# Seven block products for the output projection of a head pair, with the output's sums kept transposed in DRAM

## The chip, the cores and the metric

The kernel runs on one core of a Trainium2 chip. The metric is the device time in microseconds. A core has TensorE (PE, matmuls), VectorE (DVE), ScalarE (ACT), GpSimd (POOL) and SyncE (SP), each with its own stream of instructions that it works through in order. DMAs are issued from the streams of SP, ACT and POOL. SBUF is the on-chip memory of 128 partitions, PSUM the memory that TensorE writes, in 8 banks of 512 f32 columns.

## The reference

One block of a transformer on x of 2048 tokens by 256, all f32:

```python
xn = layernorm(x)                                   # over the 256
q, k, v = split(xn @ Wqkv.T)                        # 16 heads of 128 each
w = softmax(q @ k.T * 128 ** -0.5)                  # per head, 2048 x 2048
attn = concat_heads(w @ v) @ Wout.T                 # 2048 x 2048 -> 2048 x 256
ffn = (sigmoid(xn @ Q(w1).T) * (xn @ Q(w2).T)) @ Q(w3).T   # Q: weights to -1, 0, 1
out = x + attn + ffn
```

Softmax divides by a sum over keys; a kernel may divide after the product with V.

## The kernel before

**Tiling.** Tokens are cut into NB = 4 blocks of QB = 512; a block has TB = 4 tiles of 128 queries. A group is G = 2 heads. The attention runs over 64 blocks, block n being head n // 4, token block n % 4 (`blocks`, L586). The order of all instructions is written out by hand (`tc.manual_schedule()`, L732): each pass of the loop at L733 is a step, with u = 4n + t. A step computes scores for tile v = u + 6 (`scores`, L589) and a quarter of the weighted sum of block n (`weighted`, L652).

**A step.** TensorE makes 4 score matmuls into two PSUM tiles "s" (three exist), VectorE takes the row maxima (L607, L612), ScalarE the exps with their sums (L619). `exchanged` (L625) moves exps between partitions by 16 DMAs, 10 on SP's queue and 6 on ACT's; two steps later VectorE transposes 32x32 blocks (`transposed`, L645, L650) into pT. TensorE adds up V times pT over 16 key tiles in one PSUM bank "av" (L660), 4 of them a step. At the block's end ScalarE copies av to oT (L672).

**Products in between.** Q, K and V of later heads are made while attention runs. They come as a block matrix product of 2x2 blocks done by seven products of blocks instead of eight, from sums of weights (`weight_sums`, `v_sums`, on POOL) and of x (`x_sums`). A product is one matmul of 128x128 by 128x512 (L165, L263) into the single PSUM bank "m"; VectorE adds it into one or two results (L185 to L192, L280). In a step the first product follows the scores and its reads follow the maxima; the second follows two or three matmuls of the weighted sum and is read after the transposes. Steps t = 2, 3 do Q and K of the next head, steps t = 0 do V of the next group. V is exchanged between partitions by POOL's DMAs (L287) and transposed by VectorE (L295).

**The projection.** In step t = 1 `projected` (L676) multiplies the former block's oT, 128 queries at a time, by the head's 128x256 slice of Wout: four matmuls of 256 columns, a head at a time. VectorE scales each by the softmax's reciprocal (`inverses`, L639) and adds it into y, the running output of the token block, in one instruction (L693). y stands as [token, 256] in SBUF for one block and in DRAM between (`fetched` L715, `put_away` L721, POOL's queue).

**The front.** FFN results come out transposed (yT, L497). `added` (L500) turns them back by TensorE's transposes (L512) and adds x (L516).

Of the kernel before, what the change touches and what calls it, by code (L numbers as in the profile page):

```python
# [8 lines left out]
F32 = mybir.dt.float32  # L9
# [10 lines left out]
def layernorm_attention_bitffn_kernel(  # L20
# [51 lines left out]
    def load_weights(g: int, what: str, queue=nc.sync):  # L72

        if what == "o":
            w = wpool.tile([P, G, DM], F32, tag="wo", name=f"wo{g}")
            src = woutT[g * G * D : (g + 1) * G * D, :].rearrange("(h p) e -> p h e", p=P)
        else:
            w = wpool.tile([P, KC, G * D], F32, tag=f"w{what}", name=f"w{what}{g}")
            lo = "qkv".index(what) * HD + g * G * D
            src = wqkvT[:, lo : lo + G * D].rearrange("(c p) e -> p c e", p=P)  # L80
        queue.dma_start(w, src)
        weights[g, what] = w
# [131 lines left out]
    VH = NV // 2  # L214

    def v_piece(g: int, i: int):
# [9 lines left out]
        v = v_tile(g, i // VH).rearrange("p g k d -> p k g d")  # L226
        i = i % VH * 2
        nc.scalar.copy(v[:, i : i + 2], pm.rearrange("p k (g d) -> p k g d", g=G))

    def v_tile(g: int, half: int):  # L230
        if (g, half) not in vs:
            vs[g, half] = kvpool.tile(
                [P, G, NKT // 2, D], F32, tag="v", name=f"v{g}_{half}", bufs=4
            )
        return vs[g, half]
# [5 lines left out]
    def v_sums(g: int):  # L241
        wv = weights[g, "v"]
        w = wpool.tile([P, 4, D], F32, tag="wvs", name=f"wvs{g}")
        a, b = wv[:, :, :D], wv[:, :, D:]
        nc.gpsimd.tensor_tensor(w[:, 0], b[:, 0], b[:, 1], ALU.add)
        nc.gpsimd.tensor_tensor(w[:, 1], w[:, 0], a[:, 0], ALU.subtract)
        nc.gpsimd.tensor_tensor(w[:, 2], a[:, 0], b[:, 0], ALU.subtract)
        nc.gpsimd.tensor_tensor(w[:, 3], a[:, 1], w[:, 1], ALU.subtract)
        vws[g] = w

    def fast_v_product(g: int, m: int, second: bool):
        half, m = divmod(m, NB)
        wv, w, t = weights[g, "v"], vws[g], ts[2 * half]
# [3 lines left out]
            ((wv[:, 0, :D], x00), (w[:, 1], t[:, 1])),  # L257
            ((w[:, 2], t[:, 2]), (wv[:, 1, D:], t[:, 3])),
            ((w[:, 0], t[:, 0]), (w[:, 3], x11)),
            ((wv[:, 1, :D], x10),),  # L260
# [4 lines left out]

    def fast_v_read(g: int, m: int, second: bool, pm):
        half, m = divmod(m, NB)
        v = v_tile(g, half).rearrange("p g k d -> p g (k d)")
        a, b = (v[:, i].rearrange("p (j k r) -> p k j r", j=P // 32, r=32) for i in range(G))
        a0, a1, b0, b1 = a[:, :TB], a[:, TB:], b[:, :TB], b[:, TB:]  # L270
        pm = pm.rearrange("p (k j r) -> p k j r", j=P // 32, r=32)
        if (m, second) == (0, False):
            nc.vector.tensor_copy(a0, pm)
            return
        todo = {
            (0, True): ((a1, a0),), (1, False): ((b1, a1),), (1, True): ((b0, b1),),
            (2, False): ((b1, b1), (a1, a1)), (2, True): ((a1, a1),), (3, False): ((a0, a0),),
# [4 lines left out]
    def v_exchanged(g: int, half: int, i: int):  # L282

        v = v_tile(g, half)[:, i].rearrange("p k d -> p (k d)")
# [7 lines left out]
    def v_transposed(g: int, half: int, i: int):  # L292
        v = v_tile(g, half)[:, i].rearrange("p k (q r) -> p q k r", r=32)
# [5 lines left out]
    vws, v_part = {}, [xnT[:, 0, bass.ts(c, QB)] for c in (1, 3)]  # L299
# [5 lines left out]

    ys = [fw.tile([P, TB, DM], F32, tag=f"y{c}", name=f"y{c}") for c in range(NB)]
    away = ctx.enter_context(tc.tile_pool(name="away", bufs=1, space=bass.MemoryType.DRAM))
    yds = [away.tile([P, TB, DM], F32, tag=f"yd{c}", name=f"yd{c}") for c in range(NB)]  # L310


    def loads(fraw):
# [33 lines left out]
        for what in "ko":  # L347
            load_weights(0, what)
# [130 lines left out]
    def summed(fp, c: int, f: int):  # L479
# [14 lines left out]
        if f == FC - 1:  # L494
            yT = fp.tile([P, DM // P, QB], F32, tag="yT", name=f"yT{c}", bufs=1)
            for e in range(DM // P):
                nc.scalar.copy(yT[:, e], yTs[c][e])  # L497
            yTs[c] = yT

    def added(c: int):  # L500

        yT = yTs.pop(c)
        if c < NB - 1:
            pt = ps_s.tile([P, 2, QB], F32, tag="s", name=f"pyt{c}")
            pts = [pt.rearrange("p a (b e) -> p (a b) e", e=DM)]
        else:
            pts = [bank([P, 2, DM], f"pyt{c}_{u}") for u in range(2)]
        m = TB // len(pts)
        for u, pt in enumerate(pts):
            for t in range(m):  # L510
                for e in range(DM // P):
                    nc.tensor.transpose(  # L512
                        pt[:, t, bass.ts(e, P)], yT[:, e, bass.ts(u * m + t, P)], ident
                    )
            y = ys[c][:, u * m : (u + 1) * m]
            nc.vector.tensor_tensor(y, pt, y, ALU.add)  # L516
        nc.sync.dma_start(yds[c], ys[c])


    with tc.manual_schedule():  # L520
# [45 lines left out]
        for i, (c, f) in enumerate(chunks):  # L566
# [7 lines left out]
            if f == 3 and c:  # L574
                added(c - 1)
# [11 lines left out]
    sums, rinvs, oTs, exps, parts, pTs, avs = {}, {}, {}, {}, {}, {}, {}  # L587

    def scores(v: int, amid=None, late=None):  # L589

# [8 lines left out]
        for i in range(2):  # L599
# [9 lines left out]
            if i == 0 and amid:  # L609
                amid()  # L610
# [28 lines left out]
    def inverses(n: int):  # L639
# [3 lines left out]
        rinvs[n] = ri  # L643
# [8 lines left out]
    def weighted(n: int, k: int, part=None):  # L652
# [3 lines left out]
        if k == 0:  # L656
# [4 lines left out]
            av, vs[h // G, k // (NKT // 2)][:, h % G, k % (NKT // 2), :],  # L661
# [3 lines left out]
        if k == NKT - 1:  # L665
            oT = apool.tile([P, QB], F32, tag="oT", name=f"oT{n}_{t0}", bufs=1)
            if part == 1:

                nc.vector.tensor_copy(oT[:, :P], av[:, :P])  # L669
                nc.scalar.copy(oT[:, P : 2 * P], av[:, P:])  # L670
            else:
# [216 lines left out]
```

## Time and profile before

| | |
|---|---|
| median of 3 runs | 2254.63 us (2254.19 to 2256.97) |
| the profiled execution's own time | 2257.09 us |
| its span, first to last instruction | 2255.3 us |
| granted TensorE clock | 0.999 |
| PE, DVE, ACT, POOL busy | 2244.7, 1681.3, 692.8, 317.8 us |
| step with scores and weighted sum alone | 6.87 us |
| projection matmuls | 256 of 128x256 |
| q0 (POOL's DMAs), share of 16 DMA engines | 12.0% |

The profile names instructions by engine, line of the kernel and tiles (out<-in, buffer numbers left out). A group's row has busy time, mean ns of one, and the idle time of its engine before it with what ended that. Matmuls are pipelined: the length of one is longer than the distance to the next, so costs on TensorE are read from start to start. A timeline row gives start, length, engine, line, operation, count.

### The profile page before, as it was taken

The numbers are of one execution on the slowest core, as the hardware profiler recorded it, in microseconds if no ns is written. First come the engines' busy times: TensorE is split into PE (matmuls) and PEld (weight loads), VectorE is DVE, ScalarE is ACT, GpSimd is POOL, SyncE is SP. The second block draws the span as 40 slices with busy tenths as digits, with TensorE's granted clock in tenths as the row PEclk, the third lists the DMA queues.
The fourth block names the chain that finished last, engine by engine and source line by source line (L and its number), as shares of the span: only waits on it lengthen the run. The fifth ranks groups of instructions, "written<-read, shape, count | busy, mean of one in ns | idle before, by whom it ended". The sixth has DMA issues, their size and how long they took to land.

```text
span 2255.3 us, 24534 instructions
## 1 busy us (share of the span) xinstructions
PE 2244.7 (100%) x5754; PEld 1086.1 (48%) x5754; DVE 1681.3 (75%) x2205; ACT 692.8 (31%) x1203; POOL 317.8 (14%) x625
## 2 busy tenths in 40 slices
PE   9999999999999999999999999999999999999999
PEld 6744444444444444444444444444444444444445
DVE  6566777777777777777777777777777777777775
ACT  5533323223223223323323322322322322232331
POOL 0010000021030211203022120222103021120000
PEclk9999999999999999999999999999999999999999
DMA  2066665665665665666666665666666666666665
GB/s 95 28 164 160 171 162 147 175 176 151 166 182 152 180 174 149 177 173 167 160 175 157 176 181 147 166 179 173 168 159 174 166 174 164 157 176 173 168 170 155
DMA packets 237793, 364.73 MB, mean 162 GB/s; under 512 B 74576, under 2 KB 82192, under 8 KB 237648
## 3 DMA queue, kind: packets, MB, share of 16 engines
q1 hardware_dynamic: 131120, 178.36, 31.9%
q10 hardware_dynamic: 74704, 101.68, 17.8%
q0 software_dynamic: 31824, 83.13, 12.0%
q8 instruction: 45, 0.74, 0.1%
q14 instruction: 100, 0.82, 0.1%
HBM read 46.20 MB, written 35.65 MB: 36 GB/s over the span
## 4 chain that ended last, share of the span: by engine, by line
PE 94%; DMA 2%; SPq 1%; DVE 1%; ACT 1%; issue 0%; ACTq 0%; DVEq 0%
PE s L602 37%; PE av L660 37%; PE pw L165 7%; PE po L686 5%; PE pvw L263 3%; DMA part<-p 2%; PE ph L467 2%; PE pv L222 1%; PE pf L490 1%; SPq L634 1%; ACT p L619 0%; PE pq L115 0%; DVE pT L650 0%; PE pk L105 0%; ACTq L634 0%
## 5 line engine op out<-in xcount | busy, mean ns | idle before, releaser
L619 ACT ACTIVATE p<-s,nm 128x1024 f32<-128x1024 f32 x512 | 566.0, 1110 | 1436.8 <-DMA part<-p 986.3
L607 DVE TENSOR_REDUCE mx<-s 128x1 f32<-128x1024 f32 x512 | 626.8, 1225 | 448.8 <-PE s L602 448.6
L660 PE MATMUL av<-pT,v 128*128 128x512 f32 (+1 forms) x2080 | 940.2, 586 | 0.7 <-DVE pT L650 0.7
L602 PE MATMUL s<-kT,qT 128*128 128x512 f32 x2048 | 921.9, 592 | 1.6 <-ACT p L619 1.5
L650 DVE STREAM_TRANSPOSE pT<-part 128x1024 f32<-128x1024 f32 x512 | 604.8, 1219 | 29.4 <-DMA part<-p 27.6
L660 PEld LDWEIGHTS av<-pT,v 128*128 128x128 f32 x2080 | 395.1, 190 | 456.3 <-issue 449.9
L602 PEld LDWEIGHTS s<-kT,qT 128*128 128x128 f32 x2048 | 388.6, 190 | 464.8 <-issue 452.5
L287 POOL DMA_DIRECT2D xnT<-v x384 | 189.2, 501 | 346.5 <-DVE v L295 236.4
L721 POOL DMA_DIRECT2D yd<-ya x60 | 33.6, 560 | 735.3 <-DVE ya L693 734.0
L686 PE MATMUL po<-wo,oT 128*128 128x256 f32 x512 | 131.7, 380 | 0.6 <-DVE oT L669 0.5
L686 PEld LDWEIGHTS po<-wo,oT 128*128 128x128 f32 x512 | 97.0, 190 | 67.8 <-issue 58.4
L693 DVE SCALAR_TENSOR_TENSOR ya<-po,ri,ya 128x256 f32<-128x256 f32 x256 | 111.9, 479 | 18.0 <-issue 2.5
L619 ACT ACTIVATION_READ_ACCUMULATOR p<-s,nm 128x1 f32 x512 | 100.2, 196 | 0.0
L165 PE MATMUL pw<-t,ws 128*128 128x512 f32 x168 | 85.9, 593 | 0.0
L715 POOL DMA_DIRECT2D ya<-yd x64 | 34.3, 536 | 306.4 <-DMA yd<-ya 238.5
L188 DVE TENSOR_TENSOR kT<-pw,kT 128x512 f32<-128x512 f32 x112 | 74.7, 667 | 0.2 <-issue 0.2
L612 DVE TENSOR_REDUCE nm<-mx 128x1 f32<-128x2 f32 x256 | 39.7, 155 | 28.2 <-DVE mx L607 1.4
L185 DVE SCALAR_TENSOR_TENSOR qT<-pw,qT 128x512 f32<-128x512 f32 x84 | 57.4, 684 | 0.0
L165 PE MATMUL pw<-xnT,wk 128*128 128x512 f32 x112 | 57.2, 592 | 0.0
L280 DVE TENSOR_TENSOR v<-pvw,v 128x512 f32<-128x512 f32 x84 | 56.1, 680 | 0.0
L672 ACT COPY oT<-av 128x512 f32<-128x512 f32 x64 | 37.3, 583 | 59.2 <-PE av L660 53.6
L165 PEld LDWEIGHTS pw<-t,ws 128*128 128x128 f32 x168 | 31.6, 189 | 40.7 <-issue 33.7
(113 smaller groups left out, 784.8 us busy)
## 6 DMA issues: line engine op xcount, KB each, us to landing
part<-p SPq DMA_DIRECT2D x2560, 64.0 KB, 2.1
part<-p ACTq DMA_DIRECT2D x1536, 64.0 KB, 2.2
ya<-yd POOLq DMA_DIRECT2D x64, 512.0 KB, 4.2
yd<-ya POOLq DMA_DIRECT2D x60, 512.0 KB, 4.1
xnT<-v POOLq DMA_DIRECT2D x384, 32.0 KB, 2.6
wv<-in_wqkvT_dram SPq DMA_DIRECT2D x8, 256.0 KB, 3.6
yd<-y SPq DMA_DIRECT2D x4, 512.0 KB, 2.6
wq<-in_wqkvT_dram POOLq DMA_DIRECT2D x7, 256.0 KB, 3.7
```

The lines of the kernel that those rows point to most:

```text
L165: nc.tensor.matmul(pm, lhs, rhs, start=True, stop=True)
L185: nc.vector.scalar_tensor_tensor(q, pm, SCALE, base, ALU.mult, ALU.add)
L188: nc.vector.tensor_tensor(k, pk, base, ALU.add)
L263: nc.tensor.matmul(pm, lhs, rhs, start=True, stop=True)
L287: nc.gpsimd.dma_start(v_part[q // 2][bass.ts(j, 32), bass.ts(q % 2, S // 8)], v[bass.ts(q, 32), bass.ts(j, S // 8)],)
L602: nc.tensor.matmul(s[:, bass.ts(j, QB)], qTs[h, b][:, bass.ts(t, P)], kTs[h][:, i * HALF + j * QB : i * HALF + (j + 1) * QB], start=True, ...
L607: nc.vector.tensor_reduce(mx[:, i : i + 1], s, AX.X, ALU.max)
L619: nc.scalar.activation(p, s, AF.Exp, bias=nm, accum_out=sums[n][:, t, i : i + 1],)
L650: nc.vector.transpose(pTs[n][:, t, 2 * i : 2 * i + 2], part)
L660: nc.tensor.matmul(av, vs[h // G, k // (NKT // 2)][:, h % G, k % (NKT // 2), :], pTs[n][:, t0:t1].rearrange("p t g (k q) -> p (t g) k q", ...
L686: nc.tensor.matmul(pms[j], oTs[n, 2 * u + j], weights[h // G, "o"][:, h % G, :], start=True, stop=True,)
L693: nc.vector.scalar_tensor_tensor(y[:, t, :], pms[j], rinvs[n][:, t : t + 1], y[:, t, :], ALU.mult, ALU.add,)
```

## The change

The projection of a group's two heads is done after the group, as a product of 2x2 blocks: (two halves of the 256 outputs) x (two heads), times (two heads) x (two token blocks). Seven products of 512 columns take the place of 16 matmuls of 256. It needs the heads' outputs already divided by their softmax sums, and it gives the output's sums transposed.

- `weighted` ends in a VectorE multiply of av by rb, in place in oT. rb is the block's reciprocals spread over all partitions: `inverses` stores them to DRAM transposed (a step earlier in the program than their block begins), `spread` loads them to every partition, into oT itself. `put_away` stores oT to DRAM (`ods`).
- Group g - 1 is projected during the first head of group g, in steps t = 0, 1 of its four blocks: two token blocks (a pair) take two blocks' time. `o_fetched` loads three of the four outputs and the pair's sums (`osums`), `o_moved` makes differences on POOL, loads the fourth output and stores the sums at the end.
- The products of V move to the second head's steps t = 0, 1.
- The last group is projected per head as before, both heads summed in PSUM, in step t = 1 of the last head's blocks.
- The output's sums stand in DRAM as [output, token], starting from yT; `added` is gone. `turning_back` and `turned_back` turn them back in the last head by 16 DMAs and four VectorE transposes a block, and POOL adds x, freshly loaded.
- Wv and Wout share a buffer, as do their sums. V has three buffers of one head each, and head 1's V lies in the sums' buffer; V's copies in the first groups become two instead of one.

```diff
-        wv, w, t = weights[g, "v"], vws[g], ts[2 * half]
+        wv, w, t = weights[g, "v"], wxs[f"wvs{g}"], ts[2 * half]
...
-            for e in range(DM // P):
-                nc.scalar.copy(yT[:, e], yTs[c][e])
-            yTs[c] = yT
-
-    def added(c: int):
...
+            nc.sync.dma_start(yds[c], yT)
...
     def inverses(n: int):
         nc.vector.reciprocal(ri, ri)
-        rinvs[n] = ri
+        nc.gpsimd.dma_start(rds[n % 2].rearrange("t p -> p t"), ri)
+
+    def spread(n: int):
+
+        rb = oT
+        if n >= NBK - NB:
+            rb = kvpool.tile([P, QB], F32, tag="qT", name=f"rb{n}", bufs=NB + 2)
+        nc.gpsimd.dma_start(rb, rds[n % 2].rearrange("t p -> (t p)").partition_broadcast(P))
+        rbs[n] = rb
...
         if k == NKT - 1:
...
-                nc.scalar.copy(oT[:, : (t1 - t0) * P], av)
+            m = 1 if part == 1 else t1 - t0
+            for t in range(t0, t1, m):
+                o, rb = (a[:, t * P : (t + m) * P] for a in (oT, rbs[n]))
+                nc.vector.tensor_tensor(o, av[:, (t - t0) * P : (t - t0 + m) * P], rb, ALU.mult)
...
+    def put_away(n: int):
+        h, b = blocks[n]
+        nc.gpsimd.dma_start(ods[h % (2 * G)][b], oT)
+
+    def o_fetched(g: int, pair: int):
+        for i, (j, c) in enumerate(((0, 0), (0, 1), (1, 1))):
+            nc.gpsimd.dma_start(o3[:, i], ods[(g * G + j) % (2 * G)][2 * pair + c])
+        for c in range(2):
+            nc.gpsimd.dma_start(osums[:, c], yds[2 * pair + c])
+
+    def o_moved(g: int, pair: int, m: int):
+        o = [o3[:, i] for i in range(3)]
+        if m == 0:
+            nc.gpsimd.tensor_tensor(o[1], o[1], o[0], ALU.subtract)
+        elif m == 1:
+            nc.gpsimd.tensor_tensor(o[1], o[2], o[1], ALU.subtract)
+            nc.gpsimd.dma_start(o[2], ods[(g * G + 1) % (2 * G)][2 * pair])
+            nc.gpsimd.tensor_tensor(o[0], o[1], o[0], ALU.subtract)
+        elif m == 2:
+            nc.gpsimd.tensor_tensor(o[2], o[2], o[1], ALU.subtract)
+        elif m == 4:
+            for c in range(2):
+                nc.gpsimd.dma_start(yds[2 * pair + c], osums[:, c])
+
+    def o_parts(g: int, m: int):
...
+        return (
+            ((k[:, 0], 0, (k0, q0, k1, q1)),),
+            ((s[:, 0], 1, (k1, q1)), (s[:, 3], 2, (k1,))),
+            ((k[:, 1], 2, (k0,)), (s[:, 1], 1, (k1, q0, q1))),
+            ((s[:, 2], 0, (q0, q1)), (q[:, 1], 2, (q0,))),
+        )[m % NB]
...
+    def fast_o_read(g: int, m: int, second: bool, pm):
+        pm = pm.rearrange("p (t j r) -> p t j r", t=TB, r=32)
+        for c, e in o_parts(g, m)[second][2]:
+            y = osums[:, c, e].rearrange("p (j t r) -> p t j r", t=TB, r=32)
+            nc.vector.tensor_tensor(y, pm, y, ALU.add)
+
+    def turning_back(b: int):
...
+        for i in range(P // 32):
+            for j in range(P // 32):
+                nc.gpsimd.dma_start(
+                    part[bass.ts(j, 32), i], yds[b][bass.ts(i, 32), :, bass.ts(j, P)]
+                )
...
+    def turned_back(b: int):
...
+        for i in range(P // 32):
+            nc.vector.transpose(yv[:, i], part[:, i])
+        nc.gpsimd.tensor_tensor(sofar[b], sofar[b], yn, ALU.add)
...
+    def between(n: int, t: int):
+        g, i = divmod(n, GB)
+        last = NBK - NB
+        how = {
+            (5, 0): (v_exchanged, 0, 0), (5, 2): (v_transposed, 0, 0), (6, 1): (v_transposed, 1, 0),
+            (7, 0): (v_exchanged, 0, 1), (7, 2): (v_transposed, 0, 1),
+        }.get((i, t))
+        if how and g and g + 1 < H // G:
+            how[0]((g + 1) * G + how[1], how[2])
...
+        if t == 0:
+            if 0 < n <= last:
+                put_away(n - 1)
+        if t == 1:
+            spread(n)
...
+            if n >= last - 1:
+                b = n + 1 - last
+                nc.gpsimd.dma_start(o3[:, b % 2], ods[(H - 2) % (2 * G)][b])
...
+        b, odd = divmod(n * TB + t - (last * TB - 2), 2)
+        if not odd and 0 <= b <= NB:
+            if b:
+                turned_back(b - 1)
+            if b < NB:
+                turning_back(b)
...
-            if t == 0 and n >= GB and n // GB + 1 < H // G:
-                seven = True
-                hi = n // GB + 1, n % GB
-                product, read, twice = fast_v_product, fast_v_read, n % NB != NB - 1
+            g, i = divmod(n, GB)
+            if n >= GB and t < 2:
+                i, j = divmod(i, NB)
+                j = 2 * j + t
+                if not i:
+                    seven, hi = True, (g - 1, j)
+                    product, read, twice = fast_o_product, fast_o_read, j % NB != 0
+                elif g + 1 < H // G:
+                    seven, hi = True, (g + 1, j)
+                    product, read, twice = fast_v_product, fast_v_read, j % NB != NB - 1
...
-                    projected(n - 1, 0)
+            elif t == 1 and n > NBK - NB:
+                projected(n - 1, 0)
```

## The prediction

> **What bounds the kernel.** I read the page's busy shares first, then the chain of work that ended last, then TensorE's timeline in the steady part.
>
> ```profile
> PE 2244.7 (100%) x5754; PEld 1086.1 (48%) x5754; DVE 1681.3 (75%) x2205; ACT 692.8 (31%) x1203; POOL 317.8 (14%) x625
> ...
> PE 94%; DMA 2%; SPq 1%; DVE 1%; ACT 1%; issue 0%; ACTq 0%; DVEq 0%
> ```
>
> The first line is busy us by engine, the second the chain by engine: TensorE sets the time, VectorE is next at 75%. The timeline (start, length, engine, line, operation, count) shows whether TensorE has gaps, and what one product costs:
>
> ```profile
> 1026.71 3.60 PE L602 MATMUL s<-kT,qT 128*128 128x512 f32 x8
> 1030.15 1.03 PE L686 MATMUL po<-wo,oT 128*128 128x256 f32 x4
> 1031.01 3.60 PE L660 MATMUL av<-pT,v 128*128 128x512 f32 x8
> 1034.44 1.03 PE L686 MATMUL po<-wo,oT 128*128 128x256 f32 x4
> 1035.31 3.60 PE L602 MATMUL s<-kT,qT 128*128 128x512 f32 x8
> 1038.74 1.02 PE L165 MATMUL pw<-xnT,wk 128*128 128x512 f32 x2
> 1039.60 1.88 PE L660 MATMUL av<-pT,v 128*128 128x512 f32 x4
> ```
>
> Every f32 matmul leaves two records. From start to start, two projection matmuls of 256 columns (x4) take 1031.01 - 1030.15 = 0.86 us, so 0.43 each; one product of 512 columns (x2) takes 1039.60 - 1038.74 = 0.86. Nothing idles between, so work removed here is time removed, as long as VectorE, ScalarE and the queues keep up.
>
> **A rule weighed.** The Trainium skill, "Trainium Kernel Development and Optimization", section Performance Expectations, says that matmul busy time is a bad metric, because matmuls are pipelined, and points to weight-load busy time. PEld is at 48%, which would suggest room and so a smaller gain. The row says otherwise: there is no gap to fill, and 512 columns cost twice 256 columns, so columns are the price. The rule does correct one number: by the groups' busy time a projection record costs 131.7/512 = 0.257 us and a product record 85.9/168 = 0.511, which would give a saving of 15.1 us in the next paragraph; by spacing it is 12.0. I take the spacing.
>
> **TensorE's sum.** Groups 0 to 6 (two heads each) have two pairs of token blocks each, 14 pairs. Before, a pair costs 2 heads x 2 blocks x 4 matmuls = 16 x 0.43 = 6.87 us; after, 7 products x 0.859 = 6.01. Saved: 14 x 0.859 = 12.0 us. The last group keeps its count of matmuls (8 per block, moved to the second head's steps). The FFN result is no longer turned by TensorE: its transposes lie on the chain in the front,
>
> ```profile
> 66.55 0.87 PE pyt L512 x8
> ...
> 83.31 0.87 PE pyt L512 x8
> ...
> 100.06 0.87 PE pyt L512 x8
> ```
>
> which is 2.6 us removed where TensorE is back to back. The fourth (at 112.7) lies beside exps and exchanges of the lead-in; between 0 and 0.87, I take 0.4. TensorE sum: -15.0.
>
> **VectorE: what is added, and what hides it.** The rows (busy, mean ns, idle before):
>
> ```profile
> L287 POOL DMA_DIRECT2D xnT<-v x384 | 189.2, 501 | 346.5 <-DVE v L295 236.4
> ...
> L693 DVE SCALAR_TENSOR_TENSOR ya<-po,ri,ya 128x256 f32<-128x256 f32 x256 | 111.9, 479 | 18.0 <-issue 2.5
> ...
> L188 DVE TENSOR_TENSOR kT<-pw,kT 128x512 f32<-128x512 f32 x112 | 74.7, 667 | 0.2 <-issue 0.2
> ...
> L672 ACT COPY oT<-av 128x512 f32<-128x512 f32 x64 | 37.3, 583 | 59.2 <-PE av L660 53.6
> ```
>
> A pair's products are read into 4+3+4+3 = 14 sums of L188's kind (PSUM plus SBUF, 512 columns, 32-column pieces): 14 x 14 x 0.667 = 131 us. The normalizing multiply replaces ScalarE's copy: 64 x 0.667 = 43. Removed are 224 of L693's adds (98) and the front's adds (5). The last turning adds about 6. VectorE: 1681 + 131 + 43 - 98 - 5 + 6 = 1758 us, 78%: not the bound. But the place counts. In a step with the four-sum product (first head, t = 0) VectorE has the multiply in the gap before its first maximum (1.65 us idle there at 1020.05), then 2 x 1.23 + 0.15 for the maxima, ending 4.9 us after the step's first matmul, 4 x 0.6 (spacing of such reads in a row) to 7.4, two transposes 2.36 to 9.8. The step lasts 9 x 0.859 = 7.7 and its successor's first scores can be read at 9.5: 0.3 late, made good before the second maximum. Behind those sums wait the transposes, behind them six exchange DMAs on ScalarE's queue and the next exps; the exps' maximum comes at 7.7 + 5.1 = 12.8, and the six issues end at about 12.3. Cover: 0.5 us; without it the 14 such steps would lose up to 1 us each. In the two-product steps the second product needs the one PSUM bank back: the first read ends at 6.2, TensorE asks at 6.9. Cost taken: 0.
>
> The multiply also takes av's only PSUM bank back: VectorE is done 0.7 us after the block's last matmul, TensorE asks for the bank after four score matmuls, 3.43 us. Cost 0.
>
> **The queues.** The multiply waits for the spread reciprocals, and behind it on VectorE wait all later maxima, so TensorE too. The path is: reciprocal (step 2 of the block before), a transposing store to DRAM on POOL's queue, then, behind the put-away of the former oT, a broadcast load into oT. The store has 512 pieces of 4 bytes, which no row shows. The skill's "DMA: Bandwidth & Descriptors", section Rules for kernel authors, says that a strided last dimension becomes one descriptor per element and should be rearranged. Its bandwidth section gives about 10.5 ns per packet: an estimate of 512 x 10.5 ns = 5.4 us plus 2.0 fixed, 7.4. The nearest rows land in 2.6 us (xnT<-v, 32 rows) and 4.4 (wo, 256 rows); I take 5. Neither matters alone: put-away issues about 1 us into a block and lands in 4 (yd<-ya: 4.1), the load lands some 3 us later, and the multiply comes about 34 us into the block. In blocks with V's exchange, 16 issues of 0.5 us (L287) come first and wait for V's sums; then the load lands near 21 us. The slack is 13 us at least. By the row the charge is 0; by the rule also 0 for the wait, but 64 x 5.4 us more of DMA work; the exchange's landing (2.1 us) has some 6 us before its transpose, so that is hidden as well.
>
> POOL's order: its queue gains about 370 issues (0.54 each, 200 us) for 124 removed (68), and 56 subtractions at 1.27 (71 us, from the t<-xnT rows): about 540 us of 2240. A subtraction ends within 2.5 us of the product before it and the next product that reads it is a step away (5 us or more of slack). Loading the sums at a pair's change waits for their store to land (4 us) but has two steps, 17 us. Once, for group 0, the sums' buffer is head 1's V until its last matmul: the load's issues (1.1) and landing (4.2) end at 5.3 in a step whose reads are due at 4.9, so VectorE waits about 0.5. With the split V copies in the first blocks I charge 0.5 in all.
>
> **The end.** From the second half of block 59 to the start of block 61 there are now seven steps with scores and weighted sums only (6.87 us). ScalarE barely keeps such a pace: in the like stretch before,
>
> ```profile
> 2142.94 1.11 ACT L619 ACTIVATE p<-s,nm 128x1024 f32<-128x1024 f32 x1 [5.80 <-DMA part<-p]
> ...
> 2150.01 1.11 ACT L619 ACTIVATE p<-s,nm 128x1024 f32<-128x1024 f32 x1 [4.77 <-DVE nm L612]
> ```
>
> a round is 7.07 us with the copy, 6.5 without. In the same steps y is turned back, per block: POOL's add of 128x1024 (2.4, linear from 0.46 at 128 columns and 1.27 at 512), 17 issues x 0.5, 2.6 to land, 1.6 of VectorE's transposes: 15.1 us against two steps of 13.7. VectorE, in order, waits for it: 1.4 us later per block, and maxima, exps and scores behind it; scores have about 1 us of spare PSUM. Bounds: -1 (the wait for pT near 2242 is now covered by the moved projection) to +6; I take +2, since three of these four periods press and each has some cover.
>
> **Sum.** -15.0 + 0.5 + 2 = -12.5 us on a span of 2255.3, so 2242.8. The profiled execution took 2257.09, 1.8 more than its span; the median of the runs is 2254.63. The difference is applied to the median: 2254.6 - 12.5 = 2242.
>
> **Rivals.** *The end gives more back.* If each turning costs its full 1.4 us or more and ScalarE cannot keep 6.87, the end loses 5.5 to 10 instead of 2: 2245.6 to 2250.1. For it: ScalarE's issues stretch to 6.25 us at 2210. Against: the spare PSUM and the richer steps at blocks 61 and 62. *No change.* A small stall in each of the 14 pairs, about 0.9 us, eats the 12: the four-sum step with its 0.5 us of cover is the only place that tight. About 2250 to 2259. *Slower.* One mechanism: the reciprocals' way through DRAM is late at the multiply, so VectorE stands at each block's end and TensorE after it. The price is the lateness times 64; from 0.2 us a block the gain is gone, with 1 us it is 2242 + 64 = 2306. It decides once POOL's queue runs some 13 us behind my schedule, where 16 exchange issues precede the put-away. Against it: POOL would be busy only a quarter of the time. *A stage that does not speed up:* if the front's transposes were hidden, the gain is 2.6 smaller, inside the likeliest range.
>
> **Chances and range.** Likeliest, 0.64, with its own range of 2237.5 (fourth transposes and the end's -1 in full, and what runs differ by) to 2245.6. The end: 0.18. No change: 0.04. Slower: 0.14. The limit of 0.2% is about what a measurement of this kernel can tell from no change. Faster is 0.82. The range 2237.5 to 2250.1 takes the first two cases and leaves 0.18 out.
>
> **What would show it.** Right: projection records of 256 columns down from 512 to 64, 196 new product records spaced 0.43; no transposes in the front; TensorE without gaps from 150 to about 2130; VectorE near 1760 us. Wrong: VectorE's multiply waiting on the DMA of the spread reciprocals; gaps before second products; an end, from block 59 on, more than 4 us over its matmuls.

## The result: 8% slower

The changed kernel takes 2441.44 us (median of 5 runs, 2438.96 to 2449.42) against 2254.68 (5 runs, 2254.19 to 2256.97): a ratio of 1.083, 95% interval 1.081 to 1.085. Forecast were 2242.0 us and a range of 2237.5 to 2250.1; the result lies 191 us above its upper end. The profiled execution took 2449.42 us with a span of 2447.6, against 2257.09 and 2255.3 before.

The page of the changed kernel, busy time and then the chain by engine:

```profile
PE 2291.0 (94%) x5470; PEld 1050.1 (43%) x5470; DVE 1737.2 (71%) x2237; ACT 656.8 (27%) x1154; POOL 563.2 (23%) x968
...
PE 46%; DMA 34%; SPq 8%; DVE 5%; issue 3%; ACT 3%; ACTq 1%; DVEq 0%
```

TensorE issues 284 records fewer, as it should: 448 projection records of 256 columns gave way to 196 product records of 512, and 32 transposes are gone. It is even so busy longer, and the chain, 94% TensorE before, is now 34% DMA. The groups of the same page (busy, mean ns of one, idle before and what ended it) say where TensorE waits, and for whom:

```profile
L601 PE MATMUL s<-kT,qT 128*128 128x512 f32 x2048 | 971.4, 614 | 139.4 <-ACT p L616 139.1
L616 ACT ACTIVATE p<-s,nm 128x1024 f32<-128x1024 f32 x512 | 565.7, 1109 | 1700.0 <-DMA part<-p 1442.9
...
L730 DVE TENSOR_TENSOR osums<-pow,osums 128x512 f32<-128x512 f32 x196 | 124.6, 676 | 5.6 <-DMA osums<-yd 5.3
```

Scores wait for the exps (they need the PSUM back), and the exps for the exchange of exps, part<-p. Before, that last wait was there too, but short enough to be hidden; the list of waits of the kernel before (total us, times, longest) has

```profile
ACT p L619 <- DMA part<-p: 986.3, 178, 7.5
```

and that of the changed kernel

```profile
ACT p L616 <- DMA part<-p: 1442.9, 215, 16.4
...
PE s L601 <- ACT p L616: 139.1, 44, 7.2
```

The longest went from 7.5 us to 16.4, and a step of TensorE's work is some 8. The DMA issues (count, KB each, median us from issue to landing) of the changed kernel:

```profile
part<-p SPq DMA_DIRECT2D x2560, 64.0 KB, 2.3
...
yd<-osums POOLq DMA_DIRECT2D x28, 512.0 KB, 12.0
...
rd<-ri POOLq DMA_DIRECT2D x64, 2.0 KB, 8.7
```

and of the kernel before:

```profile
part<-p SPq DMA_DIRECT2D x2560, 64.0 KB, 2.1
```

The median exchange is nearly as quick as ever. The transposing store of the reciprocals, 2 KB in 512 pieces of 4 bytes, takes 8.7 us, longer than the median load of the output's sums, 512 KB (osums<-yd, 7.9). What it does to its neighbours is seen at one of them. Timeline of the changed kernel, POOL and ScalarE (start, length, what; in brackets the idle time before and its releaser):

```profile
1023.02 0.78 POOL L640 DMA_DIRECT2D rd<-ri  x1 [4.58 <-DVE ri L639]
...
1024.26 10.21 ACTq L631 DMA_DIRECT2D part<-p  x6
1034.72 1.11 ACT L616 ACTIVATE p<-s,nm 128x1024 f32<-128x1024 f32 x1 [10.50 <-DMA part<-p]
...
1058.42 0.78 POOL L640 DMA_DIRECT2D rd<-ri  x1 [17.02 <-DVE ri L639]
1059.20 1.09 POOL L706 DMA_DIRECT2D yd<-osums  x2
...
1059.58 15.05 ACTq L631 DMA_DIRECT2D part<-p  x6
1074.89 1.11 ACT L616 ACTIVATE p<-s,nm 128x1024 f32<-128x1024 f32 x1 [15.85 <-DMA part<-p]
...
1067.84 1.88 PE L601 MATMUL s<-kT,qT 128*128 128x512 f32 x4
1076.14 3.53 PE L601 MATMUL s<-kT,qT 128*128 128x512 f32 x4 [6.42 <-ACT p L616]
1079.51 1.02 PE L723 MATMUL pow<-o,wo 128*128 128x512 f32 x2
```

The same issues at this place in the kernel before:

```profile
1025.68 4.58 ACTq L634 DMA_DIRECT2D part<-p  x6
```

Six exchange issues of ScalarE, 3.75 to 5.05 us from 1000 to 1080 in the kernel before, take 10.2 us right after the first store and 15.1 after the second, where the stores of the output's sums come on top. ScalarE works in order, so the next two exps stand behind these issues. The first delay is nearly swallowed by the exps' lead; the second is not, and TensorE stands 6.42 us. The chain of waits shows the exchange itself, not only its issue, held as long:

```profile
1023.22 9.53 DMA part<-p
...
1058.87 9.73 DMA part<-p
1068.62 6.26 DMA part<-p
```

Stretches of the same time (length, busy us and count of PE, PEld, DVE, ACT, POOL, then granted clock, DMA share, GB/s):

```profile
1005.00:1023.00 18.00, 18.00 (x43) 7.98 (x42) 16.30 (x24) 5.67 (x10) 3.11 (x3) 1.00 0.63 165
1023.00:1033.00 10.00, 10.00 (x24) 4.37 (x23) 6.50 (x9) 1.23 (x4) 0.78 (x1) 1.00 0.63 66
1033.00:1043.00 10.00, 9.79 (x24) 4.14 (x23) 9.56 (x12) 3.81 (x7) 3.04 (x4) 1.00 0.69 166
...
1076.00:1080.00 4.00, 3.86 (x6) 1.76 (x7) 0.29 (x1) 1.19 (x3) 0.05 (x1) 0.59 1.04 356
```

In the ten us after the store the DMA engines move 66 GB/s with the same busy share that moves 165 GB/s before it. That is the store's real price. Whose packets take that time, the queues of the same ten us show (packets, MB, share of 16 engines):

```profile
q10 hardware_dynamic: 192, 0.26, 42.6%
q1 hardware_dynamic: 289, 0.39, 18.1%
q0 software_dynamic: 32, 0.00, 2.4%
```

q0 is POOL's queue, here the store alone, and q10 ScalarE's: its 101.7 MB in the whole run are the 1536 exchange issues of 64 KB. So the store's own packets take 2.4% of the engines, and the exchange's packets are the ones that last long. In the run without the store (below), q10 moves 0.46 MB in the same ten us with 17.0%.

The time can be added up. I take the start of each group of matmul records less the start of the one before and less 0.4292 us for each record of 512 columns in between, and add up what is over 0.1 us:

| | first weighted sums start at | lost to 480 us | to 200 us before the end | last 200 us | sum |
|---|---|---|---|---|---|
| before | 152.09 | 0.5 | 0 | 2.0 | 2.5 |
| after | 147.64 | 23.0 | 144.4 | 43.4 | 210.8 |

Against before: -4.5 up to the first weighted sums, -12.0 of matmul work (the prediction's figure), +208.3 of time lost: +191.8. The spans differ by 192.3. So TensorE's saving is there, and all of the loss is gaps and what comes with them.

### The profile page after: what moved, and what is told of

The parts are those of the page before. It is cut to its first block, busy times and chain, and to the rows that moved or that the text cites. A ratio compares the mean times of both kernels' runs of the same rounds, so it can differ in the third digit from the quotient of the medians.

```text
span 2447.6 us, 24044 instructions
## 1 busy us (share of the span) xinstructions
PE 2291.0 (94%) x5470; PEld 1050.1 (43%) x5470; DVE 1737.2 (71%) x2237; ACT 656.8 (27%) x1154; POOL 563.2 (23%) x968
## 3 DMA queue, kind: packets, MB, share of 16 engines
q0 software_dynamic: 41984, 101.89, 18.5%
## 4 chain that ended last, share of the span: by engine, by line
PE 46%; DMA 34%; SPq 8%; DVE 5%; issue 3%; ACT 3%; ACTq 1%; DVEq 0%
DMA part<-p 34%; PE s L601 19%; PE av L665 16%; SPq L631 8%; ACT p L616 3%; PE pow L723 3%; PE pw L166 2%; DVE pT L655 2%; PE pvw L270 2%; PE ph L485 2%; DVE mx L606 2%; ACTq L631 1%; PE pf L508 1%; PE pv L225 1%; PE pk L106 1%
## 5 line engine op out<-in xcount | busy, mean ns | idle before, releaser
L601 PE MATMUL s<-kT,qT 128*128 128x512 f32 x2048 | 971.4, 614 | 139.4 <-ACT p L616 139.1
L616 ACT ACTIVATE p<-s,nm 128x1024 f32<-128x1024 f32 x512 | 565.7, 1109 | 1700.0 <-DMA part<-p 1442.9
L665 PE MATMUL av<-pT,v 128*128 128x512 f32 (+1 forms) x1952 | 892.1, 587 | 0.5 <-DVE oT L675 0.5
L601 PEld LDWEIGHTS s<-kT,qT 128*128 128x128 f32 x2048 | 394.9, 195 | 657.1 <-issue 459.2
L665 PEld LDWEIGHTS av<-pT,v 128*128 128x128 f32 x1952 | 374.6, 192 | 460.9 <-issue 454.6
L640 POOL DMA_DIRECT2D rd<-ri x64 | 49.4, 772 | 714.1 <-DVE ri L639 706.7
L730 DVE TENSOR_TENSOR osums<-pow,osums 128x512 f32<-128x512 f32 x196 | 124.6, 676 | 5.6 <-DMA osums<-yd 5.3
L680 POOL DMA_DIRECT2D od<-oT x60 | 33.7, 561 | 263.5 <-DVE oT L675 247.9
L647 POOL DMA_DIRECT2D oT<-rd x60 | 33.0, 551 | 112.2 <-DMA od<-oT 101.6
L665 PE MATMUL av<-pT,osums 128*128 128x512 f32 x128 | 58.5, 592 | 0.0
L723 PE MATMUL pow<-o,wos 128*128 128x512 f32 x112 | 57.3, 593 | 0.0
```

Of the source, the lines that this page charges most:

```text
L601: nc.tensor.matmul(s[:, bass.ts(j, QB)], qTs[h, b][:, bass.ts(t, P)], kTs[h][:, i * HALF + j * QB : i * HALF + (j + 1) * QB], start=True, ...
L616: nc.scalar.activation(p, s, AF.Exp, bias=nm, accum_out=sums[n][:, t, i : i + 1],)
L665: nc.tensor.matmul(av, v_tile(h)[:, k, :], pTs[n][:, t0:t1].rearrange("p t g (k q) -> p (t g) k q", q=32)[:, :, k, :], start=(k == 0), sto ...
L723: nc.tensor.matmul(pm, lhs, o3[:, i], start=True, stop=True)
L730: nc.vector.tensor_tensor(y, pm, y, ALU.add)
```

## The experiments

Theory A: the store holds up the DMAs beside it, the exchange comes late, exps and scores after it. Rival B: the work put on VectorE and POOL (a multiply per block, the four-sum steps, swaps of sums) is too tight, and the DMA row is a symptom. Rival C, the prediction's own slow case: the multiply waits for the reciprocals. C has no support in the trace: the multiply (L675) waits 7.7 us in all, each time for TensorE's last matmul.

### The store taken out of the change, and put alone into the kernel before

```
         nc.vector.reciprocal(ri, ri)
-        nc.gpsimd.dma_start(rds[n % 2].rearrange("t p -> p t"), ri)
+        if n < 2:
+            nc.gpsimd.dma_start(rds[n % 2].rearrange("t p -> p t"), ri)
```

> The changed kernel with the reciprocals stored to DRAM for the first two blocks only; later blocks load those old values again, so the scaling is not the reference's, and all else is left as it is. Theory A (the store's 512 pieces of 4 bytes hold the DMA engines, the exchange of the exps stands behind them, and ScalarE and then TensorE wait): the loss of 187 us goes and the time is about 2242, at most 2250. Theory B (the store is one among many: the other new transfers of outputs and sums, and the turning back at the end, carry the loss): at least half of it stays, 2340 or more.

Measured: 2276.45 us (2273.7 to 2279.49), ratio to before 1.0086 (1.0071 to 1.0101). 165 us of the 187 are gone with 62 small DMAs. That is near A and far from B, but over the 2250 that A allowed.

```
         nc.vector.reciprocal(ri, ri)
         rinvs[n] = ri
+        nc.gpsimd.dma_start(rds[n % 2].rearrange("t p -> p t"), ri)
```

> The kernel before with one thing added: after each block's reciprocals, the same store of 512 pieces of 4 bytes to DRAM on POOL's queue, which nothing reads. Theory A: it alone makes the kernel before slower by 2 to 3 us a block, 2254 + 64 x 2.5 = about 2415, between 2380 and 2450. Theory B: without the other transfers it is hidden, 2254 to 2275.

Measured: 2419.92 us (2411.28 to 2421.68), ratio 1.0714 (1.0694 to 1.0735). Nobody reads what this store writes, nothing else of the change is there, and 163 us are lost, 2.5 us for each of 64 stores. Its group of exps and its DMA issue:

```profile
L620 ACT ACTIVATE p<-s,nm 128x1024 f32<-128x1024 f32 x512 | 566.1, 1110 | 1634.6 <-DMA part<-p 1419.1
```

```profile
rd<-ri POOLq DMA_DIRECT2D x64, 2.0 KB, 9.5
```

The waits are those of the changed kernel (1419.1 us for the exchange; 1442.9 there). So A holds for seven eighths of the loss, B and C for none of that. But without the store the change is still 19 us over before and 34 over the prediction: something else was wrong too.

### What makes the store slow: number, size, or neighbourhood of the pieces

Same bytes in 128 pieces of 16, so that each row's four values lie side by side in DRAM (the reader gets them in a wrong order):

```
-        nc.gpsimd.dma_start(rds[n % 2].rearrange("t p -> p t"), ri)
+        nc.gpsimd.dma_start(rds[n % 2].rearrange("t p -> (t p)").rearrange("(p t) -> p t", t=TB), ri)
```

> The changed kernel with the reciprocals stored as they lie, 128 pieces of 16 bytes in a row of DRAM, instead of 512 pieces of 4 bytes; the values reach the wrong queries, the traffic is the same bytes. Theory A with the number of pieces as the price: the DMA engines are held a quarter as long, about 2.5 us, which the slack of the exchange hides; 2242 to 2260. If the price is a write to DRAM as such, whatever its pieces: near 2440. Theory B: 2400 or more.

Measured: 2291.07 us (2281.93 to 2292.95), ratio 1.0143 (1.0122 to 1.0164). It lands in

```profile
rd<-ri POOLq DMA_DIRECT2D x64, 2.0 KB, 1.8
```

and 150 us are back. Number and size both changed here, so three more runs, each built on the kernel without the store, separate them. One column only, 128 pieces of 4 bytes, neighbours in DRAM as before:

```
...
+        else:
+            nc.gpsimd.dma_start(rds[n % 2][0:1].rearrange("t p -> p t"), ri[:, 0:1])
```

> From the third block on only one of the four columns of reciprocals is stored, 128 pieces of 4 bytes instead of 512; the multiplies use old reciprocals (output not the reference's). What is asked: is it the number of pieces or their size that holds the exchange? Number (128 pieces of 16 bytes cost about 15 us over the kernel without the store, which took 2276): landing near 2 us, time 2276 to 2295. Size of 4 bytes (each piece costs the same 17 ns or so whatever their number): landing near 3.5 us and, a quarter of 165 us more than without the store, about 2315.

All 512 pieces of 4 bytes, each to a place 64 bytes from the next (rws has 16 values for each one):

```
+    rws = [away.tile([TB, P, 16], F32, tag=f"rw{i}", name=f"rw{i}") for i in range(2)]
...
+        else:
+            nc.gpsimd.dma_start(rws[n % 2][:, :, 0].rearrange("t p -> p t"), ri)
```

> From the third block on the 512 pieces of 4 bytes go to places 64 bytes apart that nobody reads (the multiplies use old reciprocals, output not the reference's). If neighbouring 4-byte pieces are slow because they fall into the same 64 bytes of DRAM one after the other, the landing falls to some 3 us and the time to 2276 to 2300. If the number of pieces or their size alone is the cause, the landing stays at 8 to 10 us and the time at about 2440.

And 512 pieces of 16 bytes, 64 bytes apart (each reciprocal is the first of four values in a tile that is otherwise zero):

```
...
+        else:
+            nc.gpsimd.dma_start(rws[n % 2][:, :, :4].rearrange("t p e -> p t e"), ris[n % 2])
```

> As the run with 4-byte pieces 64 bytes apart, with 16 bytes in each of the 512 pieces (three of the four values are zeros; nobody reads them, the multiplies use old reciprocals, output not the reference's). If the number of pieces sets the cost: landing 8 to 10 us, about 2440, as with 4 bytes. If it is the size of 4 bytes: landing near 2 to 5 us, 2276 to 2330.

| | pieces | landing, us | time, us |
|---|---|---|---|
| no store | none | | 2276.45 |
| the change | 512 of 4 bytes, side by side | 8.7 | 2441.44 |
| e3_few | 128 of 4 bytes, side by side | 8.0 | 2413.93 (2413.6 to 2419.75) |
| e3_apart | 512 of 4 bytes, 64 bytes apart | 2.4 | 2291.91 (2286.45 to 2296.22) |
| e3_wide | 512 of 16 bytes, 64 bytes apart | 2.3 | 2292.69 (2288.42 to 2295.58) |
| e1_runs16 | 128 of 16 bytes, side by side | 1.8 | 2291.07 (2281.93 to 2292.95) |

The issue rows of the run with few pieces and of the run with the pieces apart:

```profile
rd<-ri POOLq DMA_DIRECT2D x62, 0.5 KB, 8.0
```

```profile
rw<-ri POOLq DMA_DIRECT2D x62, 2.0 KB, 2.4
```

A quarter of the pieces costs 137 us of the 165, where both answers foreseen lay at 2315 or less; all of them, moved apart, cost 15. The number of pieces is not it, nor the size of 4 bytes alone: it is 4-byte pieces that are neighbours in DRAM. Neighbours of 16 bytes cost no more than the pieces that are apart; 8 bytes and other distances than 64 weren't tried. The pieces are those of the program's access patterns; the trace doesn't show them. It counts 32 packets for each of these stores, whatever its pieces: POOL's queue has 41984 packets in the changed kernel and in all four variants, 40000 without the 62 stores. Why neighbours are slow is open. The Trainium skill's "DMA: Bandwidth & Descriptors", section Specifications, says that below 512 bytes the DMA reads, modifies and writes; the pieces of all five stores of the table are below that, and the three with pieces apart or of 16 bytes land in 1.8 to 2.4 us, so that alone doesn't set the price. That such accesses wait for one another where their places overlap would fit, but no row shows it.

### A store in rows, with nothing left out

VectorE turns the reciprocals (a transpose by 32x32, from a tile of 32 columns of which four are filled), and four DMAs each store 4 rows of 128 bytes:

```
-        nc.gpsimd.dma_start(rds[n % 2].rearrange("t p -> p t"), ri)
+        rt = small.tile([P, 32], F32, tag="rt", name=f"rt{n}")
+        nc.vector.transpose(rt, ris[n % 2])
+        for j in range(P // 32):
+            nc.gpsimd.dma_start(rds[n % 2][:, bass.ts(j, 32)], rt[32 * j : 32 * j + TB, :])
```

> The changed kernel with the reciprocals turned by one small VectorE transpose of 32x32 blocks and stored by four DMAs of 4 pieces of 128 bytes each, 16 pieces instead of 512; the rest is as changed. Theory A: the predicted gain comes back, 2242, perhaps 2238 to 2250 for the end; three more issues on POOL's queue a block (1.5 us) are hidden. Theory B: 2400 or more.

Measured: 2309.22 us (2304.2 to 2312.35), ratio 1.0236 (1.0219 to 1.0253): 33 us over the kernel without the store, though each DMA lands in 1.8. Its POOL timeline where the pair of blocks changes:

```profile
1004.54 2.08 POOL L646 DMA_DIRECT2D rd<-rt  x4 [17.23 <-DVE rt L644]
1006.61 1.11 POOL L712 DMA_DIRECT2D yd<-osums  x2
1007.71 1.61 POOL L695 DMA_DIRECT2D o<-od  x3
1011.50 0.53 POOL L697 DMA_DIRECT2D osums<-yd  x1 [2.17 <-DMA yd<-osums]
1014.25 0.54 POOL L697 DMA_DIRECT2D osums<-yd  x1 [2.21 <-DMA yd<-osums]
```

The store waits for VectorE's reciprocals at the head of POOL's queue, and the swap of the output's sums, long possible, stands behind it: in the kernel without the store the same swap begins right after VectorE's last sum. If that is the cause, the same stores one step later, when their data has been there for a while, do no harm:

```
+    def stored(n: int):
+        rt = rts.pop(n)
+        for j in range(P // 32):
+            nc.gpsimd.dma_start(rds[n % 2][:, bass.ts(j, 32)], rt[32 * j : 32 * j + TB, :])
...
         if t == 3:
+            stored(n + 1)
```

> The run with the turned reciprocals (16 pieces of 128 bytes), their four DMAs put one step later in POOL's queue, so that the sums' stores no longer wait behind the reciprocal. In the run with turned reciprocals 38 us of TensorE gaps lay in the second step of each group's third block, where VectorE stood for the sums to be loaded. If the place in the queue is the cause: 2309 - 33 = about 2276, as without stores. If the four small DMAs themselves are: 2300 or more.

Measured: 2280.35 us (2275.57 to 2282.62), ratio 1.0105 (1.009 to 1.012). 29 of the 33 us were the place in the queue. That the 15 us of the three stores with harmless pieces have this cause as well is argued from their like place, not tried.

### The other 34 us: the swap of sums, and the end

From the kernel without the store, once the swap of the output's sums with DRAM is left out, once the 64 DMAs that turn the result back:

```
         for c in range(2):
-            nc.gpsimd.dma_start(osums[:, c], yds[2 * pair + c])
+            if g == 0 and pair == 0:
+                nc.gpsimd.dma_start(osums[:, c], yds[2 * pair + c])
...
             for c in range(2):
-                nc.gpsimd.dma_start(yds[2 * pair + c], osums[:, c])
+                if g == H // G - 2:
+                    nc.gpsimd.dma_start(yds[2 * pair + c], osums[:, c])
```

> The run without the stores of reciprocals, with the output's sums of a pair not exchanged with DRAM either: they are loaded once and stored by the last group alone, so all pairs add into the same buffer and the output is not the reference's. Left of the run without the stores were 17 us of TensorE gaps between blocks 8 and 57, most of them at the first half of the third block of a group, where sums are stored and loaded. If that burst is their cause, they go: 2276 - 15 = about 2261. If they come from VectorE's many sums or from the loads of the outputs, it stays near 2276.

Measured: 2255.64 us (2253.76 to 2259.22), ratio 1.0000 (0.9991 to 1.0008): 21 us.

```
-        for i in range(P // 32):
-            for j in range(P // 32):
-                nc.gpsimd.dma_start(
-                    part[bass.ts(j, 32), i], yds[b][bass.ts(i, 32), :, bass.ts(j, P)]
-                )
```

> The run without the stores of reciprocals, with the 64 DMAs of the turning back at the end left out (VectorE's transposes and POOL's sums stay and work on what lies there). From block 58 on that run had 17 us of TensorE gaps against 2 in the kernel before. If the turning's transfers cause them: 2276 - 13 = about 2263. If the bare steps of scores and weighted sums alone cause them, because ScalarE cannot keep 6.87 us a step: 2272 or more.

Measured: 2264.27 us (2261.48 to 2269.15), ratio 1.0038 (1.0023 to 1.0053): 12 us by the medians (6.5 by the spans of the profiled executions, 2273.9 and 2267.4). Both of these edits at once:

> The changed kernel without the store of reciprocals after the first two blocks, without the swap of output sums with DRAM and without the 64 DMAs that turn the result back (output not the reference's). If these three are all that separates the prediction from the result, the savings of the two latter add up: 2276.5 - 20.8 - 12.2 = 2243.5, near the predicted 2242, and TensorE has hardly a gap after 150 us. If they overlap or a fourth cost is hidden behind them: 2248 to 2256.

Measured: 2251.14 us (2248.5 to 2255.86), ratio 0.9974 (0.9966 to 0.9981). The savings do not add up to 33; a fourth cost remains. Lost time of TensorE by the same working as above:

| | first weighted sums | to 480 us | middle | last 200 us |
|---|---|---|---|---|
| no store | 150.85 | 2.5 | 15.5 | 16.8 |
| no store, no swap | 150.84 | 0.4 | 0.2 | 13.7 |
| no store, no turning-back DMAs | 148.99 | 4.1 | 13.5 | 12.4 |
| none of the three | 150.91 | 2.0 | 0.2 | 11.1 |

The swap is the whole of the middle. Without it 0.2 us are left there, so in the middle the four-sum steps, the multiply and POOL's subtractions cost TensorE nothing. The end loses 11.1 us even without its DMAs, which add 2.6 (13.7 against 11.1) to 4.4 us (16.8 against 12.4). How the swap works, in the kernel without the store (POOL, ScalarE, TensorE):

```profile
990.22 1.10 POOL L707 DMA_DIRECT2D yd<-osums  x2 [10.96 <-DVE osums L731]
991.31 1.62 POOL L690 DMA_DIRECT2D o<-od  x3
994.32 0.53 POOL L692 DMA_DIRECT2D osums<-yd  x1 [1.39 <-DMA yd<-osums]
998.79 0.53 POOL L692 DMA_DIRECT2D osums<-yd  x1 [3.94 <-DMA yd<-osums]
...
997.90 9.74 ACTq L631 DMA_DIRECT2D part<-p  x6
...
1009.15 1.98 PE L601 MATMUL s<-kT,qT 128*128 128x512 f32 x4 [1.56 <-ACT p L616]
```

2816 KB go out and in within two steps (two stores and two loads of 512 KB, three loads of 256), the six exchange issues take 9.74 us, and the scores wait again. The same disease, from bytes instead of pieces. In the kernel without any of the three, the end has

```profile
2129.25 7.88 ACTq L631 DMA_DIRECT2D part<-p  x6
2137.30 1.11 ACT L616 ACTIVATE p<-s,nm 128x1024 f32<-128x1024 f32 x1 [9.28 <-DMA part<-p]
```

and in its timeline of TensorE

```profile
2138.56 2.42 PE L601 MATMUL s<-kT,qT 128*128 128x512 f32 x4 [2.43 <-ACT p L616]
...
2205.09 3.70 PE L666 MATMUL av<-pT,v 128*128 128x512 f32 x8 [2.27 <-DVE oT L676]
```

Exps are late behind a stretched exchange, and once the multiply of the block before holds the bank of av for 2.27 us, a place that the prediction priced at 0. What stretches the exchange here, with all three costs out, is open; the last store of the sums and POOL's loads of x, 512 KB each, are still there.

### A version that beats both

From the kernel with its stores one step later: groups take the two pairs in turns, so that the sums stay in SBUF at every change of group; the one swap that is left for each group goes in halves over three steps; the turning back of the first two blocks begins six and five steps earlier, of the third two steps, in buffers that V and the keys have left.

```
+    def pair_of(g: int, second: int):
+        return second ^ g % 2
...
+        if g and (i, t) == (1, 1):
+            sums_stored(pair_of(g - 1, 0), 0)
...
+            if g and i == 1:
+                o_fetched(g - 1, pair_of(g - 1, 1))
+                sums_loaded(pair_of(g - 1, 1), 0)
+                sums_stored(pair_of(g - 1, 0), 1)
...
+            (58, 0): ((turning_back, 0),), (58, 3): ((x_fetched, 0), (turned_back, 0), (turning_back, 1)),
+            (59, 1): ((x_fetched, 1), (turned_back, 1)), (60, 0): ((turning_back, 2),),
+            (60, 2): ((x_fetched, 2), (x_fetched, 3)), (60, 3): ((turned_back, 2),), 
+            (61, 0): ((turning_back, 3),), (61, 3): ((turned_back, 3),),
```

> The same as the run with the later four DMAs, and two more things: groups take their two pairs in turn in opposite order, so that the sums stay in SBUF at a group's change, and the one exchange of sums left is cut into halves over three steps; and the turning back of the first two blocks begins two blocks earlier, in other buffers. If bursts of transfers are what is left of the loss, most of the 34 us go: 2276 - 25 = about 2250, below the kernel before. If not: about 2276.

Measured: 2248.25 us (2245.85 to 2251.66), ratio 0.9968 (0.9957 to 0.998), so 0.3% under before and 193 us under the change. Which of these edits gives how much was not separated. Its page:

```profile
PE 2231.5 (99%) x5470; PEld 1035.5 (46%) x5470; DVE 1757.5 (78%) x2301; ACT 657.1 (29%) x1154; POOL 654.2 (29%) x1170
...
PE 87%; DMA 4%; SPq 1%; DVE 1%; POOL 1%; issue 0%; ACTq 0%; ACT 0%; DVEq 0%; POOLq 0%
```

The first weighted sums start at 145.45, nothing is lost until 200 us before the end, and there 16.1 us, 14 more than before. Where the DMAs that turn a block back are issued, the exchange is stretched once more:

```profile
2100.59 8.56 POOL L761 DMA_DIRECT2D back<-yd  x16
...
2104.44 6.66 ACTq L634 DMA_DIRECT2D part<-p  x6
...
2113.64 7.99 ACTq L634 DMA_DIRECT2D part<-p  x6
```

A gentler end is worth up to 14 us; it wasn't found here. Of the spans (2255.3 before, 2249.9 here) the early start alone explains 6.6 us; the saved matmuls, 12.0, are eaten by the worse end, 13.6 more lost than before.

## Why the prediction was wrong, step by step

- **TensorE's sum, -15.0: right in the matmuls, open in the front.** 12.0 us by spacing closes the account of the changed kernel to 0.5 us. The front gave 4.5 us there and 0.3 to 6.6 in the other kernels built on it, where 3.0 were taken. Part of that does not come from the change: seven kernels with the same instructions up to the first weighted sums (the changed one, four that leave something out behind them, and two with other stores) reach them between 147.6 and 151.8 us, in one execution of each. So the 3.0 are neither confirmed nor refuted.
- **VectorE, 1758 us and not the bound: right.** 1737 measured, the 196 sums at 0.676 (0.667 taken). The four-sum step, thought to have 0.5 us of cover, loses nothing (0.2 us in the whole middle without the swap).
- **POOL, about 540 us: near** (563), though the terms that the prediction gives, 318 + 200 - 68 + 71, add up to 521. The multiply's slack of 13 us held too: the slow rival, reciprocals late at the multiply, did not come true, although the result is on its side.
- **The queues: the step that failed.** "64 x 5.4 us more of DMA work; the exchange's landing (2.1 us) has some 6 us before its transpose, so that is hidden as well." The landing was bounded from 5 (by rows of other shapes) to 7.4 (an estimate by the Trainium skill's "DMA: Bandwidth & Descriptors", section Rules for kernel authors, taken with its price per packet, section Bandwidth, and its fixed 2.0 us, section Anatomy of one DMA); 8.7 was measured, outside both but near the second. A right landing would not have saved the step. It asked only who waits for the store's data, and took its work as hidden. In fact the exchange issued beside it lands after 9.5 us instead of 2.1, and the six issues on ScalarE's queue are held for 10 to 15 us: the exps behind them wait, whatever slack the transposes have. Ten us of delay against 6 of slack leave some 4 us a block (an estimate from these two numbers), where the run with the store alone shows 2.5, 163 in all. The page's rule, to avoid a strided last dimension, speaks against the change and I heard it, but priced it by the number of pieces; the runs show that the number is not the price, and the trace has 32 packets where 512 were priced.
- **Swaps of sums, "two steps, 17 us", cost 0: wrong by 21 us.** The time until the sums are needed was enough (L730 idles 5.6 us in all); what their 2816 KB do to the exchange was not asked. It is the same omission.
- **The end, +2, bounds -1 to +6: wrong.** It loses 14.8 us more than before in the kernel without the store, 9.1 without any of the three costs. The rival with 5.5 to 10 was nearer. In place of a wait of VectorE for the turning, it is mostly ScalarE's exps behind stretched exchange issues: in the kernel without the store scores wait 8.8 us for exps in the last 200 us, and a weighted sum once 3.0 us for the multiply that holds av's bank.

With the terms as measured: 2242 + 165 (store) + 21 (swap) + 12.8 (end, 14.8 in place of 2) = 2440.8; 2441.4 was measured. Four forecasts of the experiments failed as well. Without the store 2250 at most was expected and 2276 measured: the swap and the end were not seen yet. The run with few pieces fell outside both of its answers. The stores in 16-byte pieces and in rows were to be free, and cost 15 and 33 us; for the rows 29 of the 33 were the place in front of the swap, where the store waits for its data and the swap behind it.

## What to carry to other kernels

Price a DMA that is added beside an exchange whose landing others wait for by what it does to that exchange's landing and to the issues of the engine that starts it, not only by who waits for its data; compare the GB/s of the stretch beside it with those before. Don't store a column of single 4-byte values to neighbouring addresses: turn it first, or leave space between, and issue it only when its data is there, since whatever follows on its queue waits too. Choose an order of work in which large sums need not move, and move the rest in halves over several steps (the two were tried only together).

## What the runs showed of the chip

- **4-byte neighbours.** 128 stores of 4 bytes side by side take 8.0 us and cost 137 us over 62 blocks; 512 of them 64 bytes apart take 2.4 and cost 15.
- **The clock halves at long gaps.** The stretch from 1076 to 1080 has a granted clock of 0.59: after the gap that ended at 1076.14 four score records take 1079.51 - 1076.14 = 3.37 us, where four take 4 x 0.43 = 1.72. The changed kernel's granted clock falls to a half in 25 stretches, 143 us in all; the kernel before has none between its first 13 us and its last, the kernel without the store one, of 3.4 us. All 21 gaps of 3.5 us and more have such a stretch at their end, and so have four of the eight gaps of 2.1 to 2.8; three gaps of 2.1 to 3.1 in the kernel without the store have none. The Trainium skill's "TensorE: Matmul & The Clock Gate", section Part 1: The HAM clock gate, tells of such a fall after an idle window of some 3.4 us; the longer gaps agree, and the four short ones show that less idle time can do. So a late DMA is paid twice. The stretches begin within the gaps, and TensorE works in 101 of the 143 us, so the halved clock costs some 50 us (an estimate, half of 101). Records that start later than they should, with no gap before them, add up to 56 us. Of the 208 us lost some 50 to 56 are clock, and the rest, over 150, waiting.
